# Layers 1 to 3 of a four-layer image network: one-level Strassen products on four PSUM pairs, attention in double steps, and reciprocals of gathered denominators

## The chip, the cores and the metric

The kernel runs on one core of a Trainium2 chip. A core has five engines that work side by side and wait for each other by semaphores: TensorE (PE) multiplies matrices out of SBUF into PSUM, VectorE (DVE) and ScalarE (ACT) work elementwise on SBUF and PSUM, GpSimd (POOL) works on SBUF, and SyncE (SP) issues transfers. PSUM has eight banks; a bank holds 512 float32 numbers in each of 128 partitions. The metric is the device time of one execution in microseconds, as the median of several runs. Everything is float32.

## The reference

The input x has 2 images of 512 channels and 32 x 32 pixels; each of four layers adds something to it. Layer 0 is attention with 64 sampled keys and a bias computed by a small network, followed by an MLP (512 to 2048 to 512); the change does not touch it. The three other layers, cut to what is computed:

```python
# layer 1: group norm, 8 heads of 64 channels, 1024 x 1024 scores per head
h = group_norm(x);  q, k, v = split(qkv_w @ h + qkv_b)
w = softmax(q.T @ k / 8);  x = x + proj_w @ (v @ w.T) + proj_b
# layer 2: group norm, one head of 512 channels
h = group_norm(x);  q, k, v = split(w_qkv @ h + b_qkv)
a = softmax(q.T @ k / sqrt(512));  x = x + w_proj @ (v @ a.T) + b_proj
# layer 3: no norm, queries and keys of 64 channels, values of 512
q, k, v = wq @ x + bq, wk @ x + bk, wv @ x + bv
x = x + gamma * (v @ softmax(q.T @ k, axis=1))
```

## The kernel before

The program is written out in full, without loops on the chip. The function `layers` runs after `layer0` and holds layer 0's MLP and then layers 1 to 3. A helper (`in_order`) makes each engine execute its instructions in the order in which they are written, so a wait at the head of an engine's queue holds everything behind it. Python generators (`advance`, `drain`) weave two pieces of work together in that order.

Channels lie on partitions, in four chunks of 128 (CC = 4), and the 1024 pixels of an image along the free dimension, in two halves of 512. `accumulate` (L135 in the profile) is a chain of matmuls into one PSUM region: each takes a 128 x 128 stationary block and a 128 x 512 moving block. The trace shows every matmul of the program as two records, because float32 goes through the array in two passes.

The order after the MLP is as follows.

- Layer 1: `project` (L1315, tile pm) makes queries and keys of two heads at a time with stationary blocks of 64 columns, in pairs on the two halves of the array; `values` (L135, pmv) makes the transposed values. The loop over 65 steps (image, pair of heads, block of 128 keys) writes the scores of one block for both heads (L1426, contraction over 64 rows, the two heads in pairs), takes exponentials on ACT (L1427), and multiplies the exponentials of the step before with the values (L1474, pv). DVE sums the exponentials (L1357). `divide` sums those over partitions with a matrix of ones (den, L1374), copies, inverts 128 x 1024 numbers (L1377) and multiplies. The next pair's projections and the output projection (`add_projection`, L1346) are woven into the steps.
- Layer 2 for each image: `project` with a folded weight g2 (t), `values` with a folded weight v2, eight score blocks (score2, L135) with exponentials (L1561), then `weigh` (pw2, L135): products of values and exponentials, each multiplied by the reciprocal of the denominators (L1532) and added to x (L1533).
- Layer 3 for each image: `project_both` (L1574), values, scores, `weigh`, and the store of the output.

PSUM is divided among three pools: two banks of `ps_m` for projections and the like, two pairs of banks for scores, one pair for pv. The MLP already uses one-level Strassen (Winograd's form with seven products and fifteen additions): `lefts`, `rights`, `products` and `combined`. There all seven products of a 128 x 128 output are written into two PSUM tiles before ACT and DVE read any of them. Before layer 3's end a `flag` is computed from the extreme reciprocals (`note`); if it is not zero, a slower general version of the three layers runs again.

Of the kernel before, what the change touches and what calls it, by code (L numbers as in the profile page):

```python
# [11 lines left out]
F32 = mybir.dt.float32  # L12
# [6 lines left out]
P = 128  # L19
B, C, H, W = 2, 512, 32, 32  # L20
HW = H * W
# [58 lines left out]
def kernel(ctx: ExitStack, tc: tile.TileContext, a: dict, out: bass.AP):  # L80
# [971 lines left out]
    def layers(f, fold_d, t2_b, o2_b):  # L1052
# [5 lines left out]
        chan = f.enter_context(tc.tile_pool(name="chan", bufs=4))  # L1058
        ps_m = f.enter_context(tc.tile_pool(name="ps_m", bufs=2, space=PSUM))
# [9 lines left out]
        NSUM = 12  # L1069
# [3 lines left out]
        def group_norm(x, gname, bname, out):  # L1073
# [9 lines left out]
            def over_group(v, name):  # L1083
                pg = ps_m.tile([P, CC], F32, name="pg", tag="mm")
                nc.tensor.matmul(pg, cs("gmean"), v, start=True, stop=True)
                g = small.tile([P, CC], F32, name=name)
                nc.vector.tensor_copy(g, pg)
                return g
# [25 lines left out]
            yield  # L1114
            for cc in range(CC):
                hc = chan.tile([P, HW], F32, name="hc", tag="chan")
                nc.gpsimd.tensor_scalar(  # L1117
                    hc, x[:, cc, :], sc[:, cc : cc + 1], sh[:, cc : cc + 1], ALU.mult, ALU.add
                )
                out.append(hc)  # L1120
            yield

        GN_STATS = CC + 3

        h1s, h2s = [[], []], [[], []]
        norm = group_norm(xs[0], "gn_w", "gn_b", h1s[0])
# [3 lines left out]
        with ExitStack() as mlp:  # L1130
# [124 lines left out]
            for blk in range(1, NBLK):  # L1255
# [21 lines left out]
                if blk + 1 < NBLK:  # L1277
                    right1 = normed_rights(blk + 1)
                else:
                    qkv1, proj1 = load_w(wa, "wa", [a["qkv1_w"], a["proj1_w"]])  # L1280
# [20 lines left out]
        drain(norm)  # L1301


        qkp = f.enter_context(tc.tile_pool(name="qkp", bufs=4))
        ps_s = f.enter_context(tc.tile_pool(name="ps_s", bufs=2, space=PSUM))
        ps_v = f.enter_context(tc.tile_pool(name="ps_v", bufs=1, space=PSUM))

        def project(w, lo, h, bias, r, wide):

            for half in range(2):  # L1310
                n = slice(half * HALF, (half + 1) * HALF)
                pm = ps_m.tile([P, HALF], F32, name="pm", tag="mm")
                for k in range(CC):
                    for at in range(0, P, wide):
                        nc.tensor.matmul(  # L1315
                            pm[at : at + wide],
                            w[:, k, lo + at : lo + at + wide],
                            h[k][:, n],
                            start=(k == 0),
                            stop=(k == CC - 1),  # L1320
                        )
                    if k == 1:
                        yield
                nc.scalar.activation(r[:, n], pm, AF.Identity, bias=bias)
                yield

        def values(w, h, vT, bias=None, scale=None):

            for s in range(8):
                pm = ps_m.tile([P, C], F32, name="pmv", tag="mm")  # L1330
                accumulate(pm, [(h[k][:, s * P : (s + 1) * P], w[:, k, :]) for k in range(CC)])
                if bias is not None:
                    nc.vector.tensor_add(vT[:, s, :], pm, bias)
                elif scale is not None:
                    nc.scalar.mul(vT[:, s, :], pm, scale)
                else:
                    nc.scalar.copy(vT[:, s, :], pm)
                yield

        def add_projection(x, w, bname, o):  # L1340
            for half in range(2):
                n = slice(half * HALF, (half + 1) * HALF)
                for m in range(CC):
                    pm = ps_m.tile([P, HALF], F32, name="ppr", tag="mm")
                    for k in range(CC):
                        nc.tensor.matmul(  # L1346
                            pm, w[:, k, m * P : (m + 1) * P], o[k][:, n], start=(k == 0), stop=(k == CC - 1)
                        )
                        if k == 1:
                            yield  # L1350
                    nc.vector.scalar_tensor_tensor(x[:, m, n], pm, col(bname, m), x[:, m, n], ALU.add, ALU.add)
                    yield

        def summed(acc, p, first):

            if first is None:
                nc.vector.tensor_add(acc, acc, p)  # L1357
            else:
                nc.vector.tensor_add(acc, first, p)  # L1359
# [6 lines left out]
        def divide(o, acc):  # L1366

            r = rp.tile([P, HW], F32, name="r")
            for half in range(2):
                n = slice(half * HALF, (half + 1) * HALF)  # L1370
                den = ps_m.tile([P, HALF], F32, name="den", tag="mm")
                for part in range(2):
                    q = slice(part * 64, part * 64 + 64)
                    nc.tensor.matmul(den[q], ones[:, :64], acc[:, part, n], start=True, stop=True)  # L1374
                nc.scalar.copy(r[:, n], den)
                yield
            nc.vector.reciprocal(r, r)  # L1377
            nc.vector.tensor_mul(o, o, r)
            note(r)
            yield  # L1380

        def reciprocals_of_both(acc):

            r = rp.tile([P, HW], F32, name="r")
            den = ps_v.tile([P, HW], F32, name="den2", tag="pv")
            for half in range(2):
                n = slice(half * HALF, (half + 1) * HALF)
                accumulate(den[:, n], [(ones, acc[:, part, n]) for part in range(2)])
                nc.scalar.copy(r[:, n], den[:, n])
                nc.vector.reciprocal(r[:, n], r[:, n])  # L1390
            return r

        wb_stack.close()
        fold2 = f.enter_context(tc.tile_pool(name="fold2", bufs=1))
        vbias = fold2.tile([P, C], F32, name="vbias")
        nc.sync.dma_start(out=vbias, in_=a["vb"][0].partition_broadcast(P))
        g2, v2 = [fold2.tile([P, CC, C], F32, name=name) for name in ("g2", "v2")]
        for w, j in ((g2, 0), (v2, 1)):
            nc.sync.dma_start(out=w, in_=fold_d[j])
        outs = f.enter_context(tc.tile_pool(name="outs", bufs=5))  # L1400

        vp = f.enter_context(tc.tile_pool(name="vp", bufs=1))
        pp_ = f.enter_context(tc.tile_pool(name="pp", bufs=4))
        accp = f.enter_context(tc.tile_pool(name="accp", bufs=1))
        rp = f.enter_context(tc.tile_pool(name="rp", bufs=1))

        def new_v():
            return vp.tile([P, 8, C], F32, name="vT")


        def qk1(h, m):
            q = qkp.tile([P, HW], F32, name="q", tag="qk")
            k = qkp.tile([P, HW], F32, name="k", tag="qk")
            yield (q, k)
            yield from project(qkv1, m * P, h, col("qkv_b", m), q, 64)
            yield from project(qkv1, C + m * P, h, col("qkv_b", CC + m), k, 64)

        def exponentials(qs, ks, left, scale):

            p = pp_.tile([P, 2, HW], F32, name="p")  # L1420
            for half in range(2):
                n = slice(half * HALF, (half + 1) * HALF)
                sc = ps_s.tile([P, 2, HALF], F32, name="score", tag="s")
                for part in range(2):
                    r = slice(part * 64, part * 64 + 64)
                    nc.tensor.matmul(sc[:, part, :], ks[part][r, left[part]], qs[part][r, n], start=True, stop=True)  # L1426
                nc.scalar.activation(p[:, :, n], sc, AF.Exp, scale=scale)  # L1427
            return p

        qk_steps = qk1(h1s[0], 0)  # L1430
        qk = next(qk_steps)
        drain(qk_steps)
        vT = new_v()
        drain(values(qkv1[:, :, 2 * C : 3 * C], h1s[0], vT, bias=vbias))
        norms = [
            group_norm(xs[1], "gn_w", "gn_b", h1s[1]),
            group_norm(xs[0], "gn2_w", "gn2_b", h2s[0]),
            group_norm(xs[1], "gn2_w", "gn2_b", h2s[1]),
        ]
        os_ = [[], []]  # L1440
        more = iter(())
        dividing = iter(())
        late = None
        for i in range(65):
            b, m, s = i // 32, i // 8 % 4, i % 8
            if i < 64:
                if s == 0:
                    if i:
                        drain(qk_steps)
                        qk = qk_next  # L1450
# [265 lines left out]
```

## Time and profile before

| | |
|---|---|
| median of 3 runs | 3491.22 us (3489.61 to 3491.63) |
| span of the profiled execution | 3487.9 us |
| layer 0 attention, up to 2160 us; MLP up to 2451.7 us | 2451.7 us |
| layers 1 to 3, 2451.7 us to the end | 1036.2 us |
| busy in the span: PE, DVE, ACT, POOL | 99%, 71%, 50%, 14% |

The profiled execution's span is 3.3 us under the median of the runs. A share of 99% for PE says that the array seldom waits, not that each of its instructions is needed; in layers 1 to 3 the waits of PE for other engines come to 7.4 us. The granted TensorE clock is 1.00 there (0.99 in the last stretch). All numbers of the prediction are made against the 3487.9 us span and carried over to the median by adding 3.3 us.

### The profile page before, as it was taken

How to read it: one execution, taken by the hardware profiler on the slowest of the kernel's cores; microseconds unless marked ns; L12 is line 12 of the kernel's file. 1: busy time of each engine (PE TensorE's matmuls, PEld its weight loads, DVE VectorE, ACT ScalarE, POOL GpSimd, SP SyncE). 2: the span in 40 equal slices, each digit the busy share in tenths (PEclk: the TensorE clock that was granted, in tenths of full speed). 3: DMA queues.
4: the chain of work that ended last, by engine and by line, in shares of the span. 5: the costliest groups of instructions: out<-in, count | busy, mean ns of one | idle time of the engine just before them, and what ended most of it. 6: DMA issues, size and time to landing. Idle time of an engine off the chain costs nothing.

```text
span 3487.9 us, 58691 instructions
## 1 busy us (share of the span) xinstructions
PE 3452.8 (99%) x24257; PEld 1446.9 (41%) x24257; DVE 2474.8 (71%) x2733; ACT 1754.7 (50%) x2479; POOL 491.4 (14%) x579
## 2 busy tenths in 40 slices
PE   9999999999999999999999999999999999999999
PEld 4333333333333233333333369999433333444443
DVE  6999999999997999999999845455264374130223
ACT  4767867867765867768676612112243242011111
POOL 0222222222221222222222200000001000000000
PEclk9999999999999999999999999999999999999999
DMA  5776676666774666766676620001000000000000
GB/s 167 151 148 143 135 154 140 148 146 139 150 149 91 145 147 131 151 141 143 151 149 141 135 95 10 13 13 56 34 1 0 1 0 0 15 0 0 6 30 25
DMA packets 134068, 313.65 MB, mean 90 GB/s; under 512 B 21152, under 2 KB 66592, under 8 KB 133024
## 3 DMA queue, kind: packets, MB, share of 16 engines
q0 software_dynamic: 56880, 199.79, 30.1%
q1 hardware_dynamic: 75616, 105.31, 9.5%
q8 instruction: 193, 3.16, 0.4%
q10 hardware_dynamic: 1296, 4.72, 0.3%
q14 instruction: 83, 0.68, 0.1%
HBM read 65.17 MB, written 10.75 MB: 22 GB/s over the span
## 4 chain that ended last, share of the span: by engine, by line
PE 78%; DVE 16%; issue 4%; ACT 2%; DMA 0%; POOL 0%; DVEq 0%; SPq 0%; ACTq 0%; POOLq 0%
PE z L542 33%; PE pw L135 6%; DVE wa L525 6%; PE pm L1315 5%; PE pma L135 5%; PE pmv L135 5%; DVE h L556 5%; PE pmb L135 4%; PE score L1426 4%; PE score L135 3%; PE pv L1474 3%; DVE h L525 2%; PE ppr L1346 2%; PE pmp L135 2%; PE pp L628 1%
## 5 line engine op out<-in xcount | busy, mean ns | idle before, releaser
L542 PE MATMUL z<-wa,cpb_w 128*32 128x512 f32 x11904 | 1779.1, 593 | 6.6 <-DVE simbias L489 3.4
L551 ACT ACTIVATE h<-z,b2h 128x1024 f32<-128x1024 f32 x1024 | 1134.4, 1114 | 529.7 <-PE z L542 506.2
L542 PE MATMUL z<-h,cpb_w 128*32 128x512 f32 x4480 | 986.3, 593 | 3.3 <-ACT h L551 2.2
L525 DVE CUSTOM_DVE_ANT_1 wa<-tab,tab 128x1024 f32<-128x1024 f32 x744 | 878.4, 1216 | 34.0 <-PE z L542 33.9
L542 PEld LDWEIGHTS z<-wa,cpb_w 128*32 128x32 f32 x11904 | 492.9, 110 | 883.7 <-issue 805.5
L556 DVE SCALAR_TENSOR_TENSOR h<-h,turn,h 128x1024 f32<-128x1024 f32 x512 | 653.5, 1276 | 8.8 <-ACT h L551 8.6
L542 PEld LDWEIGHTS z<-h,cpb_w 128*32 128x32 f32 x4480 | 256.3, 110 | 335.0 <-issue 291.8
L831 POOL DMA_DIRECT2D h<-h x255 | 226.5, 888 | 1071.0 <-DVE h L556 697.4
L525 DVE CUSTOM_DVE_ANT_1 h<-tab,tab 128x1024 f32<-128x1024 f32 x280 | 333.0, 1216 | 10.5 <-PE z L542 10.4
L1427 ACT ACTIVATE p<-score 128x1024 f32<-128x1024 f32 x144 | 139.5, 1021 | 184.8 <-PE score L1426 184.8
L135 PE MATMUL pw<-p,vT 128*128 128x512 f32 x512 | 221.8, 593 | 1.3 <-DVE y L1532 1.3
L1357 DVE TENSOR_TENSOR acc<-acc,p 128x2048 f32<-128x2048 f32 x56 | 128.8, 2300 | 105.1 <-ACT p L1427 57.8
L1210 ACT COPY p<-pma 128x128 f32<-128x128 f32 x70 | 18.5, 265 | 304.2 <-PE pma L135 304.2
L824 POOL DMA_DIRECT2D h<-h x126 | 108.7, 863 | 343.5 <-DMA h<-h 339.8
L1359 DVE TENSOR_TENSOR acc<-p 128x2048 f32<-128x2048 f32 x12 | 27.5, 2291 | 182.4 <-ACT p L1561 108.8
L135 PEld LDWEIGHTS pw<-p,vT 128*128 128x128 f32 x512 | 97.0, 190 | 122.6 <-issue 121.0
L1202 DVE TENSOR_TENSOR upper<-pma,p 128x256 f32<-128x256 f32 x70 | 29.5, 422 | 163.3 <-ACT p L1210 163.3
L828 POOL DMA_DIRECT2D h<-h x126 | 121.9, 968 | 117.9 <-DMA h<-h 111.4
L1426 PE MATMUL score<-q,k 64*128 64x512 f32 x512 | 127.2, 615 | 0.0
L1117 POOL TENSOR_SCALAR hc<-x,sc,sh 128x1024 f32<-128x1024 f32 x16 | 27.5, 1728 | 704.4 <-DVE sh L1113 507.8
L1315 PE MATMUL pm<-hc,wa 128*64 128x512 f32 x512 | 122.4, 603 | 0.0
L1474 PE MATMUL pv<-p,vT 128*64 128x512 f32 x512 | 121.4, 595 | 0.0
(320 smaller groups left out, 3239.7 us busy)
## 6 DMA issues: line engine op xcount, KB each, us to landing
h<-h POOLq DMA_DIRECT2D x255, 512.0 KB, 4.8
h<-h POOLq DMA_DIRECT2D x252, 256.0 KB, 4.9
tab<-slog_d SPq DMA_DIRECT2D x128, 256.0 KB, 4.5
h<-h SPq DMA_DIRECT2D x126, 256.0 KB, 2.3
xt<-in_xt SPq DMA_DIRECT2D x8, 512.0 KB, 7.6
wa<-in_mlp_w SPq DMA_DIRECT2D x4, 1024.0 KB, 7.9
wb<-in_mlp_w SPq DMA_DIRECT2D x16, 256.0 KB, 5.6
x_d<-x SPq DMA_DIRECT2D x32, 128.0 KB, 1.8
```

Of the source, the lines that this page charges most:

```text
L135: nc.tensor.matmul(pm, w, m, start=(k == 0), stop=(k == len(pairs) - 1))
L525: nc.vector._custom_dve(TENSOR_ADD_SAT, out=h1.rearrange("p (y x) -> p y x", x=W), in0=tx[:, quad, point, :].unsqueeze(1).to_broadcast([P, ...
L542: nc.tensor.matmul(z[point * 32 : point * 32 + 32, n], cpb_w2[:, lo : lo + 32], h1s[point][:, n], start=True, stop=True,)
L551: nc.scalar.activation(h2, z, AF.Relu, bias=b2h[:, part : part + 1])
L556: nc.vector.scalar_tensor_tensor(h2, h2, turn[:, part // 2 : part // 2 + 1], parts.pop(part + 1), ALU.mult, ALU.add)
L828: nc.gpsimd.dma_start(out=joins[i - 3][1:P:2], in_=joins.pop(i - 2)[1:P:2], accum_op=ALU.add)
L831: nc.gpsimd.dma_start(out=joins[i - 1], in_=other, accum_op=ALU.add)
L1315: nc.tensor.matmul(pm[at : at + wide], w[:, k, lo + at : lo + at + wide], h[k][:, n], start=(k == 0), stop=(k == CC - 1),)
L1357: nc.vector.tensor_add(acc, acc, p)
L1426: nc.tensor.matmul(sc[:, part, :], ks[part][r, left[part]], qs[part][r, n], start=True, stop=True)
L1427: nc.scalar.activation(p[:, :, n], sc, AF.Exp, scale=scale)
L1474: nc.tensor.matmul(pv[part * 64 : part * 64 + 64, n], vT[:, ls, lo : lo + 64], lp[:, part, n], start=(ls == 0), stop=(ls == 7),)
```

## The change

Layer 0 and the MLP keep their instructions, but for the way in which layer 1's weights are loaded. Layers 1 to 3 are rewritten:

- Every large product except the per-head attention is split one level by Strassen: the two operands are cut into 2 x 2 blocks, sums of blocks are formed (`left_sums`, `right_sums`, eight additions), and seven block products replace eight. `group` does one such unit. It takes two PSUM tiles of two banks each, xy and vz (regions x, y, v, z of one bank each), out of a pool of four such pairs, which now serves everything. In `group`, ACT copies x (p1) after the first product and v (p5) after the third, DVE adds u2 and u3, and further products accumulate onto what lies in x, y and v. The moving block is 512 wide (n = HALF) in q/k, t and output projections, and 256 wide (n = QUARTER) in values, score2, pw2 and pw3. The first unit of layer 1 is done without Strassen (`plain`).
- The projections of all heads come before the attention of an image, with 128-column stationary blocks. `attend` has 17 steps of two key blocks; its scores use the four pairs too.
- `divide` copies the sums, moves one row per head into a compact 128 x 16 tile by DMA, inverts that, writes it to DRAM and reads it back spread over 64 partitions.
- In layers 2 and 3 the sums of exponentials are added on GpSimd (`grow`). In layer 3 the exponentials are divided before the sums of blocks are formed (`shared`): GpSimd multiplies four 128 x 1024 tiles, and DVE forms four additions for each.
- The work is staggered by hand: for instance `shared` stands between the two units of a weighed product.

```diff
-        ps_s = f.enter_context(tc.tile_pool(name="ps_s", bufs=2, space=PSUM))
-        ps_v = f.enter_context(tc.tile_pool(name="ps_v", bufs=1, space=PSUM))
...
+        banks = f.enter_context(tc.tile_pool(name="banks", bufs=4, space=PSUM))
...
+        def pair(name):
+            return banks.tile([P, 2, HALF], F32, name=name, tag="pair")
...
+        def right_sums(b11, b12, b21, b22, t1, t2, t4, t3=None):
+
+            nc.vector.tensor_tensor(t1, b12, b11, ALU.subtract)
+            nc.vector.tensor_tensor(t2, b22, t1, ALU.subtract)
+            nc.vector.tensor_tensor(t4, b21, t2, ALU.subtract)
+            nc.vector.tensor_tensor(b12 if t3 is None else t3, b22, b12, ALU.subtract)
...
+        def group(name, nk, n, stationary, moving, evict, plain=False):
+
+            xy, vz = pair(name), pair(name)
+            x, y, v, z = xy[:, 0, :n], xy[:, 1, :n], vz[:, 0, :n], vz[:, 1, :n]
...
+            add(x, 0, 0)
+            p1 = temp("p1", n)
+            nc.scalar.copy(p1, x)
+            add(y, 5, 5)
+            u2 = temp("u2", n)
+            nc.vector.tensor_tensor(u2, y, p1, ALU.add)
+            add(v, 4, 4)
+            p5 = temp("p5", n)
+            nc.scalar.copy(p5, v)
+            add(z, 3, 3)
+            add(x, 1, 1, False)
+            add(y, 6, 6, False)
+            u3 = temp("u3", n)
+            nc.vector.tensor_tensor(u3, y, p1, ALU.add)
+            add(v, 2, 2, False)
+            evict((x, None), (v, u2), (z, u3), (p5, u3))
...
+            for i in range(17):
+                m, sp = divmod(i, 4)
...
+                    for s in (2 * sp, 2 * sp + 1):
+                        for half in range(2):
+                            n = slice(half * HALF, (half + 1) * HALF)
+                            sc = pair("score")
...
+                            nc.scalar.activation(p, sc, AF.Exp, scale=64 ** -0.5)
...
+            nc.vector.reciprocal(few, few)
+            note(few)
+            d = sums_d.tile([P, HW // 64], F32, name="d")
+            nc.sync.dma_start(out=d, in_=few)
...
+            def grow(self, c):
+                p = self.score(c)
+                self.p.append(p)
...
+                    nc.gpsimd.tensor_tensor(self.acc, self.p[0] if c == 1 else self.acc, p, ALU.add)
+
+            def divisor(self):
...
+                accumulate(den, [(ones, acc[:, k]) for k in range(2)])
+                self.r = temp("r", HALF)
+                nc.vector.reciprocal(self.r, den)
+                note(self.r)
+
+            def normalize(self, c):
+                y = self.p[c].rearrange("p (k n) -> p k n", k=2)
+                nc.gpsimd.tensor_tensor(y, y, self.r.unsqueeze(1).to_broadcast([P, 2, HALF]), ALU.mult)
...
+            def form(self, c):
...
+                right_sums(*self.parts(c))
...
+            def shared(self):
+                self.divisor()
+                for c in range(4):
+                    self.normalize(c)
+                for c in range(4):
+                    self.form(c)
...
+                def evict(c11, c12, c21, c22):
+                    q = [p[:, i * QUARTER : (i + 1) * QUARTER] for i in range(4)]
+                    nc.scalar.activation(q[0], c11[0], AF.Exp, scale=C ** -0.5)
+                    put(q[2], c21)
+                    put(q[3], c22)
+                    put(q[1], c12)
+                    nc.scalar.activation(p[:, QUARTER:], p[:, QUARTER:], AF.Exp, scale=C ** -0.5)
...
+        steps = weighed("pw3", xs[0], 0, seven_v, a0, gb3, store(0))
+        advance(steps)
+        a1.shared()
+        seven_x = pixels3(xs[1])
+        both = project_both(xs[1])
+        drain(steps)
...
+        steps = weighed("pw3", xs[0], 1, seven_v0, a1, gb3, store(0))
+        advance(steps)
+        b0.shared()
+        drain(steps)
+        for c in range(4):
+            b1.grow(c)
+        steps = weighed("pw3", xs[1], 0, seven_v, b0, gb3, store(1))
+        advance(steps)
+        b1.shared()
+        checks = guard()
+        advance(checks)
+        drain(steps)
+        steps = weighed("pw3", xs[1], 1, seven_v, b1, gb3, store(1))
```

## The prediction

> **What bounds the kernel now.** I read first the busy time by stage (columns: stretch in us, its length, then busy us of PE, PEld, DVE, ACT, POOL, granted clock, DMA share, GB/s), with stages cut where the chain of waits changes its lines.
>
> ```profile
> 2451.70:2493.30 41.60, 41.60 (x131) 16.64 (x130) 7.10 (x13) 4.30 (x6) 0.00 (x0) 1.00 0.17 64
> 2493.30:2908.50 415.20, 411.85 (x1673) 135.57 (x1673) 234.09 (x161) 157.62 (x179) 17.64 (x8) 1.00 0.00 1
> 2908.50:2991.10 82.60, 82.60 (x194) 36.68 (x194) 15.29 (x11) 10.76 (x17) 0.00 (x0) 1.00 0.00 0
> 2991.10:3276.70 285.60, 282.87 (x663) 124.83 (x663) 61.95 (x71) 31.86 (x40) 4.72 (x4) 1.00 0.02 5
> 3276.70:3487.90 211.20, 203.83 (x530) 84.83 (x530) 56.17 (x54) 34.30 (x44) 0.00 (x0) 0.99 0.08 26
> ```
>
> Layers 1 to 3 take 1036.2 us and PE is busy in 1022.8 of them: PE's own instructions bound the stage, and DVE and ACT have much room. The chain in order of time gives their rates, free of overlap (start, us, line, records):
>
> ```profile
> 2433.86 5.36 PE pmb L135 x48
> ...
> 2493.28 1.92 PE score L1426 x8
> 2495.19 1.87 PE pm L1315 x8
> ...
> 2506.35 1.72 PE pv L1474 x8
> ...
> 3057.32 34.35 PE pw L135 x80
> ```
>
> Two records are one matmul: 0.859 us for a moving block of 512 (34.35/40), 0.223 for 128 (5.36/24), so 0.43 for 256 by the line between them. A score matmul costs 0.48, a pv one 0.43, a 64-column projection 0.467.
>
> Last, the order of time around the one place where PE writes the second bank of a two-bank tile after ACT has read the first:
>
> ```profile
> 3326.51 1.88 PE L135 MATMUL den<-acc,ones 128*128 128x512 f32 x4
> ...
> 3328.43 0.58 ACT L1389 COPY r<-den 128x512 f32<-128x512 f32 x1 [7.89 <-PE den L135]
> ...
> 3329.07 1.98 PE L135 MATMUL den<-acc,ones 128*128 128x512 f32 x4 [0.68 <-ACT r L1389]
> ...
> 3330.89 3.17 PE L135 MATMUL pw<-p,vT 128*128 128x512 f32 x7
> ```
>
> PE waits although the banks differ. Eight records took 4.38 us (3326.51 to 3330.89) where 8 x 0.429 = 3.43 are needed: **one such round trip costs 0.95 us**, 0.585 of it the copy.
>
> **The change part by part.**
>
> *1. Fewer products.* Before, the PE rows of layers 1 to 3 add up to 1019: q/k 256 x 0.467 = 119.7; values 165; t and output projections 110; score2 110; pw 220; attention scores, pv and den 248; layer 3's scores and projections 29; den of layers 2 and 3 17.5. After, I count in the built order 226 matmuls of 512 (193.9), 1008 of 256 (432.4), 288 scores (138.2), 256 pv (110), 32 den (15.4), 16 wide den (13.7) and 32 projections of layer 3 (14): 917.6. Saved: 102 us. A 256-wide matmul costs at least 0.429 (half of 512) and, held up by its weights, at most 2 x 0.223 = 0.446: up to 17 us for the range.
>
> *2. New round trips.* In the built order the first matmul of y waits for the copy p1 that reads x, and the first of z for p5 that reads v: these are the two banks of one tile, as in den above. PE stands still twice in each of 71 units. Fifteen units have n = 512: 30 x 0.95 = 28.5. Fifty-six have n = 256; ACT's PSUM copy takes 0.265 at 128 and 0.585 at 512, so 0.37 at 256, and a trip 0.95 - 0.21 = 0.74: 112 x 0.74 = 82.9. Sum: **111.4 us**. A unit of n = 256 and two blocks then takes 6.02 + 1.48 = 7.5 against 6.87 for the eight products that it replaces. The ends are 73 (the idle time alone, 0.68 at 512 and so 0.47 at 256) and 135 (0.95 for each of the 142).
>
> *3. Exponentials in front of p1.* In score2 ACT's queue holds the exponential of 768 elements (0.85, between 0.50 for 256 and 1.02 for 1024) before the next unit's p1, and it waits for three DVE additions (3 x 0.42) after the unit's last matmul. It ends 2.35 after that matmul; p1 could have started at 1.0. So +1.4 for each of 16 units: 22 us (13 to 30).
>
> *4. `shared`, four times.* DVE's queue: eviction of the unit before (3 x 0.42 and 2 x 0.75, so 3), reciprocal of 512 (3.32), two reductions (0.7 each), then 16 additions of 256 (0.42) that wait for four GpSimd products, and only then u2 of the second unit, for which PE's x waits. A GpSimd tensor-by-tensor operation has no row. The nearest is a one-input pass over 128 x 1024, from the POOL's order of time:
>
> ```profile
> 2418.99 5.10 POOL L1117 TENSOR_SCALAR hc<-x,sc,sh 128x1024 f32<-128x1024 f32 x4 [41.46 <-DVE sh L1113]
> ...
> 2868.91 8.63 POOL L1117 TENSOR_SCALAR hc<-x,sc,sh 128x1024 f32<-128x1024 f32 x4 [239.14 <-DVE sh L1113]
> ```
>
> That is 1.28 alone and 2.16 beside DVE's two-input sums. Lower bound 1.28 (same speed), upper 4.3 (both inputs at the contended rate); I take two uncontended passes, 2.55. Then u2 is ready 3 + 3.3 + 4 x 2.55 + 1.7 + 0.4 = 18.6 after the first unit's end; PE could use it at 1.7 (den) + 4 x 1.72 + 2 x 0.74 = 10.1. It waits 8.5, and about 10 with additions and products in each other's way; the a1 call has 7 us of other PE work ahead but 5 of pixel sums on DVE. In all 38 us (17 to 72).
>
> The Trainium skill, GPSIMD Engine Reference, "Performance versus the Vector engine", gives 4497 ns for a two-input addition of 2048 float32 elements, so an estimate of 2.25 us for 1024, which would make part 4 about 5 us smaller; it advises VectorE for such work, which speaks against this part of the change. Its page SBUF — State Buffer, "Who interferes with whom", says that a GpSimd instruction reading SBUF and a VectorE one with two SBUF inputs exclude each other; the 2.16 beside 1.28 agrees, and full exclusion would add some 5 us per call.
>
> *5. Attention in double steps.* Scores, pv and den cost PE the same. A double step is 3.84 + 3.44 = 7.3 us of PE; in it ACT has four exponentials (4.1), DVE four additions (4 x 1.19 = 4.8), so both stay covered, and three score pairs beside pv suffice: the fourth score starts at 2.9, the first exponential ends at 2.2. Start and end: 2.5 for each image. The value bias moves from DVE (16 x 0.69) to GpSimd behind the division: nothing, since the next unit waits for it only in part 7.
>
> *6. Compact inversion.* Removes 8 x 6.55 of reciprocals and 8 x 2.4 of reductions from DVE, nearly all beside PE; before, it showed as 2.2 us of waiting at 2906. It adds five DMAs per pair on SP's queue, which has nothing else there, but DVE's product now waits at the head of its queue for two trips (landing 2 to 4.5 us each by the page's rows). In `attend` one double step lies between: zero. After the last pair in the second image only one value unit does: 4 us.
>
> *7. Seams.* Beginning with the MLP's last tiles 1; sums of value blocks before each of four weighed products 1.7 each; den between score units, with its reciprocal on DVE, 4.5 per image; pixel sums and group norm 2.2; loading of layer 3's weights behind the release of layer 2's is covered by a 13.5 us unit. With parts 5 and 6: 28 us (10 to 60). The tail after the last product, 6.2 before, stays.
>
> *Sum:* 917.6 + 111.4 + 22 + 38 + 28 + 6 = 1123, against 1036.2: +87. Span 2451.7 + 1123 = 3574.7; plus 3.3 for the median: **3578 us**.
>
> Part 4's waits are the longest; before, the longest wait of PE here is 2.2 us, and the granted clock stays at 1.00 or 0.99. The Trainium skill, TensorE: Matmul & The Clock Gate, "The HAM clock gate", says that the clock halves after an idle window of some 3.4 us; no run here shows it, and by it an estimated 2 us per call would come on top, 3586.
>
> **Rivals.** A, my forecast: the round trips eat the saving (102 against 111) and the rest is loss. B, faster: the copies hide, because a wait on the other bank is not paid as in den. Then 917.6 + 22 + 38 + 28 + 6 = 1012, 24 us less, 3467. For it speaks that ACT is idle most of the stage; against it den's row, and that the copy alone lasts 0.37. It decides where a trip costs under 0.17 us: (111.4 - 87)/142. C, much slower: GpSimd products at 4.3 and in DVE's way, so that `shared` costs 18 each and score units stretch by 2: 1123 + 34 + 32 = 1189, 3644. D, the flag fires and the general layers run too: thousands of us; the data give no reason. E, the split saves less than it says (256-wide products held up by weight loads): 17 us more, 3595, inside the range.
>
> **How the numbers follow.** A with E 0.75, C 0.15, B 0.09, D 0.01. A and E alone: part 1 up to 17, part 2 from 73 to 135, part 3 from 13 to 30, part 4 from 17 to 72, part 7 from 10 to 60. All low give 1037 and all high 1238, 3492 and 3693; they are independent, so half of each distance, 3535 to 3635. Taking in half of C makes 3525 to 3640; below it lies B, above it the worst of C and D. A kernel like this is told from no change beyond about 0.2% (7 us): faster 0.08, same 0.03, slower 0.89.
>
> **What would show it.** Right: PE idle in layers 1 to 3 rises from 13 us to over 150; PE waits for p1 and p5 head the list of waits, 71 each, 0.5 to 0.7 us idle; score2 units start 8.9 us apart, value units 7.5; DVE works through `shared` while PE waits for u2 four times. Wrong: y starting right after x; GpSimd products near 1.3; PE busy well above 930.

## The result and the profile after

The changed kernel takes 3609.03 us (median of 4 runs, 3607.79 to 3612.62), the kernel before 3490.57 (3489.61 to 3491.63): a ratio of 1.0341, 95% interval 1.0326 to 1.0356. It is slower by 118 us; the forecast was 3578, 87 slower. The profiled execution has a span of 3606.0 us, of which layers 1 to 3 take 1154.7 instead of 1036.2.

Busy time by stage of the changed kernel (columns as in the prediction; rows 1 and 2: projections and attention of the first image; 3 and 4: the first output projection, then the same of the second image; 5 and 6: the second output projection and layer 2; 7: the end of layer 2 and layer 3):

```profile
2451.30:2539.60 88.30, 77.92 (x231) 42.12 (x230) 31.41 (x50) 12.80 (x26) 0.00 (x0) 1.00 0.01 3
2539.60:2661.10 121.50, 121.15 (x541) 42.70 (x540) 84.77 (x101) 70.51 (x76) 20.28 (x7) 1.00 0.08 23
2661.10:2782.40 121.30, 105.87 (x292) 52.96 (x290) 37.58 (x65) 16.26 (x30) 7.31 (x4) 0.99 0.03 7
2782.40:2903.90 121.50, 121.15 (x541) 42.72 (x540) 91.53 (x109) 69.30 (x74) 24.56 (x10) 1.00 0.10 31
2903.90:2980.60 76.70, 66.25 (x178) 31.18 (x177) 31.87 (x53) 10.31 (x18) 7.28 (x4) 1.00 0.03 7
2980.60:3290.00 309.40, 248.44 (x975) 181.02 (x975) 161.97 (x304) 48.94 (x107) 43.85 (x20) 0.98 0.02 5
3290.00:3606.00 316.00, 242.22 (x986) 174.76 (x986) 162.82 (x256) 41.37 (x77) 67.39 (x29) 0.92 0.05 17
```

Before, PE was busy in 99% of layers 1 to 3; now it stands still in every stage except attention, for 171.7 us in all (1154.7 less 983.0), and in the last stage it also runs at a lower clock. The waits of PE there (total us, times, longest):

```profile
PE pw L1356 <- DVE u L1376: 45.5, 5, 12.5
PE score L1356 <- ACT p L1373: 23.8, 16, 6.1
PE pmv L1356 <- ACT p L1373: 14.1, 24, 1.5
PE pmv L1356 <- ACT p L1379: 11.9, 24, 0.5
...
PE score L1356 <- ACT p L1379: 7.8, 16, 0.5
PE pw L1356 <- DVE vs L1332: 7.0, 7, 1.8
```

All lines with p together (L1373 is p1, L1379 is p5) make 95.5 us in 142 waits; u makes 59.0, of which `shared` has 44.8 in four waits of 12.5, 8.6, 11.3 and 12.5 us. One unit of values in order of time shows both round trips; 12 of the last row's 16 records are its own, so the next unit starts at 2516.7 and this one takes 7.56 us (forecast 7.5):

```profile
2509.13 1.03 PE L1356 MATMUL pmv<-wa,hc 128*128 128x256 f32 x4
2510.67 1.99 PE L1356 MATMUL pmv<-wa,h1t 128*128 128x256 f32 x8 [0.52 <-ACT p L1373]
2513.13 1.13 PE L1356 MATMUL pmv<-wa,h1t 128*128 128x256 f32 x4 [0.46 <-ACT p L1379]
2514.10 3.62 PE L1356 MATMUL pmv<-wa,hc 128*128 128x256 f32 x16
```

And one call of `shared`, first POOL's line, then DVE's, then PE's:

```profile
3335.85 9.61 POOL L1767 TENSOR_TENSOR p<-p,r 128x1024 f32<-128x1024 f32 x4 [14.06 <-DVE r L1762]
```
```profile
3332.42 3.35 DVE L1762 RECIPROCAL r<-den 128x512 f32<-128x512 f32 x1
...
3338.24 2.55 DVE L1338 TENSOR_TENSOR pt<-p 128x256 f32<-128x256 f32 x1 [1.16 <-POOL p L1767]
3340.82 2.44 DVE L1339 TENSOR_TENSOR pt<-p,pt 128x256 f32<-128x256 f32 x1
3343.30 2.45 DVE L1340 TENSOR_TENSOR pt<-p,pt 128x256 f32<-128x256 f32 x1
3345.67 0.41 DVE L1341 TENSOR_TENSOR p<-p 128x256 f32<-128x256 f32 x1
...
3350.76 0.42 DVE L1376 TENSOR_TENSOR u<-pw,p 128x256 f32<-128x256 f32 x1
```
```profile
3336.74 1.99 PE L1356 MATMUL pw<-pt,vT 128*128 128x256 f32 x8 [0.52 <-ACT p L1379]
3351.24 6.19 PE L1356 MATMUL pw<-p,vT 128*128 128x256 f32 x16 [12.51 <-DVE u L1376]
```

PE waits 12.5 us for one addition of 0.42 us that stands behind everything else in DVE's queue. While GpSimd multiplies (9.61/4 = 2.4 us each), DVE's additions last 2.44 to 2.55 us instead of 0.42. After the wait the 16 records of PE take 6.19 us; in the value unit above, 16 took 3.62.

### The profile page after: what moved, and what is told of

Read it like the earlier page. It is cut to its first block, busy times and chain, and to the rows that moved or that the text cites. A ratio compares the mean times of both kernels' runs of the same rounds, so it can differ in the third digit from the quotient of the medians.

```text
span 3606.0 us, 61030 instructions
## 1 busy us (share of the span) xinstructions
PE 3413.1 (95%) x24805; PEld 1615.9 (45%) x24805; DVE 2701.4 (75%) x3360; ACT 1785.3 (50%) x2600; POOL 639.6 (18%) x640
## 4 chain that ended last, share of the span: by engine, by line
PE 70%; DVE 19%; issue 6%; ACT 4%; POOL 1%; DMA 0%; DVEq 0%; SPq 0%; ACTq 0%; POOLq 0%
PE z L542 32%; DVE wa L525 6%; PE pma L135 5%; DVE h L556 4%; PE pmb L135 4%; PE pmv L1356 4%; PE pw L1356 4%; PE pv L1514 3%; PE score L1500 3%; PE pm L1356 3%; DVE h L525 2%; PE score L1356 2%; PE pmp L135 2%; PE pp L628 1%; PE pmt L1356 1%
## 5 line engine op out<-in xcount | busy, mean ns | idle before, releaser
L1504 ACT ACTIVATE p<-score 128x1024 f32<-128x1024 f32 x128 | 120.6, 1033 | 76.8 <-PE score L1500 76.4
L1356 PE MATMUL pw<-p,vT 128*128 128x256 f32 x384 | 97.5, 408 | 45.5 <-DVE u L1376 45.5
L1535 DVE TENSOR_TENSOR acc<-acc,p 128x1024 f32<-128x1024 f32 x96 | 114.2, 1251 | 27.8 <-ACT p L1504 27.8
L1500 PE MATMUL score<-q,k 64*128 64x512 f32 x512 | 118.5, 602 | 0.7 <-ACT p L1504 0.7
L1356 PE MATMUL pmv<-wa,hc 128*128 128x256 f32 x384 | 94.4, 390 | 16.1 <-DVE u L1376 8.1
L1356 PEld LDWEIGHTS pw<-p,vT 128*128 128x128 f32 x384 | 77.9, 206 | 65.5 <-DVE u L1376 47.5
L1567 POOL TENSOR_SCALAR o<-o,vb 128x1024 f32<-128x1024 f32 x8 | 30.7, 3832 | 401.9 <-DVE o L1566 231.8
L512 ACT ACTIVATE tab<-tab,pc 128x512 f32<-128x512 f32 x126 | 96.2, 763 | 0.0
```

The source lines that it names most:

```text
L1356: nc.tensor.matmul(out, stationary(l, k), moving(r, k), start=start and k == 0, stop=k == nk - 1, skip_group_check=not start,)
L1500: nc.tensor.matmul(sc[:, part, :], ks[m][r, s * P : (s + 1) * P], qs[m][r, n], start=True, stop=True)
L1504: nc.scalar.activation(p, sc, AF.Exp, scale=64 ** -0.5)
L1535: nc.vector.tensor_add(acc[half], acc[half], ps[s, half])
```

## The experiments

The kernel before had medians of 3490.1 to 3491.6 us beside these runs, so its time moved by 0.04%. "Slow clock" in the table counts the groups of 256-wide records in layers 1 to 3 that ran over by more than 0.3 us: what they took beyond 0.216 us for each record and 0.17 at the group's end. Waits are PE's, from the profiled execution of each.

| run | median us | waits for p | waits for u | slow clock |
|---|---|---|---|---|
| the change | 3609.0 | 95.5 | 59.0 | 16.6 |
| e1 other pairing | 3587.2 | 9.3 | 123.6 | 49.1 |
| e2 `shared` spread | 3579.1 | 95.8 | 28.2 | 14.3 |
| e3 exponential behind p1 | 3600.8 | 81.3 | 62.1 | 21.2 |
| e9 product on DVE | 3599.0 | 95.4 | 47.5 | 18.1 |
| e5 = e1 + e2 + e3 | 3533.0 | 2.9 | 84.0 | 34.0 |
| e6 = e5, forms two late | 3528.8 | 2.9 | 78.3 | 30.7 |
| e4 eight products | 3474.1 | 0 | 0 | 0 |
| e7 eight, no sums | 3477.5 | 0 | 0 | 0 |
| e8 seven where DVE is free | 3456.9 | 0.8 | 18.7 | 5.1 |
| e10 = e8, sums behind u2 | 3444.1 | 0.8 | 7.5 | 0 |

**1. The other pairing of the banks.**

```diff
-            xy, vz = pair(name), pair(name)
-            x, y, v, z = xy[:, 0, :n], xy[:, 1, :n], vz[:, 0, :n], vz[:, 1, :n]
+            xv, yz = pair(name), pair(name)
+            x, v, y, z = xv[:, 0, :n], xv[:, 1, :n], yz[:, 0, :n], yz[:, 1, :n]
```

> One line of `group` is changed: x and v share a two-bank tile, and y and z the other; every instruction stays and keeps its place. Theory (round trips): y then need not wait for p1, nor z for p5; the copies run beside the product on the other tile. The 142 waits of 0.46 to 0.73 us for p1 and p5 go, with 111.4 us by the forecast's prices; up to 0.1 us each may come back where v waits for p1 or z for u2 (14 us), and the score units lose a part of what the late p1 costs (10 of 22). 95 to 125 us faster than the changed kernel, 3484 to 3514. Rival 1 (the stops belong to the array's change of bank or of operands, and the trace only puts the copy's name on them): less than 20 us faster, above 3589. Rival 2 (the gaps only move, to u2 and u3): 20 to 60 us faster, with as many waits for u as there were for p.

Measured: 3587.2 us (3582.0 to 3588.5), 22 us faster than the change, where the theory asked for 95 or more. The mechanism was right, though: without any change of order the waits for p fell from 95.5 to 9.3 us, and a value unit runs through in 6.05 us instead of 7.56:

```profile
2506.97 3.62 PE L1356 MATMUL pmv<-wa,hc 128*128 128x256 f32 x16
2510.43 2.75 PE L1356 MATMUL pmv<-wa,h1t 128*128 128x256 f32 x12
2513.02 3.62 PE L1356 MATMUL pmv<-wa,hc 128*128 128x256 f32 x16
2516.47 2.75 PE L1356 MATMUL pmv<-wa,h1t 128*128 128x256 f32 x12
```

So a trip costs (7.56 - 6.05)/2 = 0.755 us (forecast 0.74), and it belongs to the tile, not to the bank or to the array. PE's idle time is 0.49 of it. The other 0.27 is 0.17 at the end of the group before the wait and 0.10 because the records after it start slower (8 of them take 1.99 us instead of 1.89). PE's stops for u and vs in the change pay the same 0.27. The Trainium skill, PSUM — Partial Sum Buffer, "PSUM bank collisions raise a hardware error", says that accesses of two engines to different banks run clean; this run agrees, since ACT now copies out of one bank beside PE's product in another: the wait came from the program, which orders accesses by tile.

What the theory missed is rival 2, though not in its form: there are 31 waits for u, up to 15.4 us long, not as many as there were for p. In layers 2 and 3 PE now comes earlier to a DVE that is no earlier: the waits for u rise by 64.6 us. And the clock falls more often: in this kernel's score units of layer 2, 12 records behind waits of 0.40 and 1.98 us take 4.6 us, and the granted clock (the column before the last two) is 0.50 for 3.4 us there,

```profile
3171.56 1.13 PE L1356 MATMUL score<-ts,h2t 128*128 128x256 f32 x4 [0.40 <-ACT p L1373]
3174.67 1.53 PE L1356 MATMUL score<-t,h2t 128*128 128x256 f32 x4 [1.98 <-DVE u L1376]
3176.00 3.22 PE L1356 MATMUL score<-t,hc 128*128 128x256 f32 x8
```
```profile
3175.30:3178.70 3.40, 3.40 (x10) 2.69 (x9) 0.00 (x0) 0.00 (x0) 0.00 (x0) 0.50 0.00 0
```

where 8 such records take 1.89 at full clock. The account closes to 2 us: 86.2 less of waits for p, 30 less at 114 fewer stops (0.27 each), 64.6 more for u, 32.5 more of slow clock, 1.2 more of others: 18 us less, against 19.3 between the two profiled spans.

**2. `shared` spread over later units.** DVE's additions (`form`) leave `shared`; a0's and a1's go behind the value units that follow, b0's and b1's behind the units of the product before, whose calls start one unit earlier.

```diff
             def shared(self):
                 self.divisor()
                 for c in range(4):
                     self.normalize(c)
-                for c in range(4):
-                    self.form(c)
...
         for c in range(4):
             advance(value_steps)
+            a0.form(c)
             a1.grow(c)
```

> `shared` now holds only the denominators and the four GpSimd products; DVE's sixteen additions stand behind later units, by ones or twos, and the last two calls begin one unit earlier. Theory (DVE's queue holds u2 behind additions that wait for GpSimd): the four waits of 8.6 to 12.5 us for u2 (44.8 us) and the slow clock after each (16 records in 5.2 to 6.2 us instead of 3.6, so 8.6 us) go; up to 3 us each may come back where a product starts before the last sums are there: 40 to 53 us faster than the changed kernel, 3556 to 3569. Rival (the work of GpSimd and DVE itself is the limit, since the two exclude each other, and the wait moves to the next product): 0 to 15 us faster, above 3594, with waits of 8 us or more elsewhere.

Measured: 3579.1 us (3576.2 to 3581.0), 30 us faster; neither theory nor rival. Three of the four long waits went, and waits of 0.4 to 2.1 us stand in their place. One of 9.6 us stayed, in the product with a1, whose u2 stands behind sums of value blocks and b0's denominators, and its cause is what the rival said. DVE's order of time in this kernel, while GpSimd multiplies (3474.13 to 3483.9):

```profile
3475.28 1.48 DVE L1331 TENSOR_TENSOR wa<-vT 128x256 f32<-128x256 f32 x1
3476.80 2.44 DVE L1332 TENSOR_TENSOR wa<-wa,vT 128x256 f32<-128x256 f32 x1
3479.28 2.44 DVE L1333 TENSOR_TENSOR wa<-vT,wa 128x256 f32<-128x256 f32 x1
3481.65 2.56 DVE L1334 TENSOR_TENSOR vT<-vT 128x256 f32<-128x256 f32 x1
3484.13 0.41 DVE L1331 TENSOR_TENSOR wa<-vT 128x256 f32<-128x256 f32 x1
```

These are sums of value blocks that wait for nothing of GpSimd's, and each still takes as long as one GpSimd product. So two causes add up in `shared`: the place in DVE's queue, and that DVE's additions of two SBUF operands get through only between GpSimd's instructions.

**3. The exponential behind p1.**

```diff
-                    nc.scalar.activation(p[:, QUARTER:], p[:, QUARTER:], AF.Exp, scale=C ** -0.5)
+                    pending.append(
+                        lambda: nc.scalar.activation(p[:, QUARTER:], p[:, QUARTER:], AF.Exp, scale=C ** -0.5)
+                    )
...
             nc.scalar.copy(p1, x)
+            while pending:
+                pending.pop(0)()
```

> In layer 2's score units the exponential of 768 elements, and the addition of the tile on GpSimd, are written behind the copy p1 of the next unit. Theory (ACT's queue holds p1 behind an exponential that waits for DVE): score units fall from 8.5 us to about 7.3; 16 times 1.4 is 22 us, 16 to 26 us faster than the changed kernel, 3583 to 3593. Rival (p1 waits for something else, as the release of PSUM or of temporary tiles): 0 to 6 us faster, above 3603.

Measured: 3600.8 us (3600.5 to 3604.6), 8 us faster: between the theory's 16 to 26 and the rival's 0 to 6. The theory's cause holds and its size does not. Undisturbed score units fall from 8.5 to 7.55 us, because PE's wait for p1 falls from 1.46 to 0.52 us: p1 was late by 0.94 us, not by 1.4, and in 11 score units, not in all 16. In all, 14 us of waits for p went, and 3 us of waits for u and 5 us of slow clock came. One wait for p1 of 6.1 us, which was a single event beside the group norm of the second image, fell to 4.0. ACT's order of time in the changed kernel says why:

```profile
3046.41 0.84 ACT L1824 ACTIVATE p<-p 128x768 f32<-128x768 f32 x1 [1.15 <-DVE p L1397]
3047.28 1.28 ACT L1102 ACT_TABLE_LOAD   x1
3050.42 0.21 ACT L1102 ACTIVATE rs<-var 128x4 f32<-128x4 f32 x1 [1.86 <-DVE var L1099]
3050.64 1.28 ACT L1103 ACT_TABLE_LOAD   x1
3051.94 0.21 ACT L1103 ACTIVATE rs<-rs 128x4 f32<-128x4 f32 x1
3052.05 0.35 ACT L1373 COPY p<-score 128x256 f32<-128x256 f32 x1
```

The copy p1 stands behind two functions of the norm with a table load of 1.28 us each, and the first of them waits for DVE, whose addition was just held up for 2.56 us beside GpSimd's sum of exponentials.

**4. Eight products.** `group` always takes its branch without p1, p5, u2 and u3; the fourth sum of each set, which overwrites an operand, is not formed. In this kernel the two off-diagonal blocks of the value units and of layer 2's score units stand in each other's place; the amount of work is the same.

```diff
-            if plain:
+            if True:
```

> All units use the branch `plain`: eight block products instead of seven, no p1, p5, u2 and u3, and of each four sums of blocks the three that overwrite nothing are still formed, though not read. Theory: PE gets 27 us more of 512-wide and 62 us more of 256-wide matmuls, and loses 111 us of round trips, 22 us of late p1 and 54 us of `shared` (nothing of the next unit waits on DVE): 90 to 125 us faster than the changed kernel, 3484 to 3519, so that Strassen's form costs here more than the eighth product that it saves. Rival (the loss lies in the restaging, the sums and the seams, not in the form of the unit): about 89 us slower, 3680 to 3700, or between the two.

Measured: 3474.1 us (3472.8 to 3475.7): 135 us faster than the change, 10 more than the theory's upper end, and faster than the kernel before (ratio 0.9953, 0.9936 to 0.9970). PE waits 2.9 us in all of layers 1 to 3:

```profile
PE pm L1354 <- DVE upper L1207: 2.2, 1, 2.2
PE score L1499 <- ACT p L1503: 0.7, 2, 0.3
```

So Strassen's form as written costs here 135 us more than it saves, and the restaging (the new order of projections, attention and divisions) is no loss. The table accounts for it: waits for p 95.5, waits for u 59.0, 7 of other waits, 44 at 166 fewer stops (0.27 each) and slow clock 16.6, less 89 for the eighth products, make 133 of the 133.6 us between the two profiled spans.

**5 and 6. The three edits together, and the forms later still.** The sixth run also moves, in `score_blocks`, each `form` one score unit further back.

> The edits of the first three experiments together. Alone they took 22, 30 and 8 us off the changed kernel (3609), so by addition 3549. Theory (with the other pairing PE no longer waits for ACT's copies but for DVE, whose queue holds u2; in that run the waits for u rose from 59 to 122 us, 64 of them in pw): the spread sums of `shared` then free more than alone, because PE comes to them earlier: pw's waits fall from 64 to some 20 us, and the slow clock after the waits goes with them: 3515 to 3535. Rival (the pairing only exposes DVE's total work, which stays): 3545 or more.

> As the run before (three together), and in layer 2 the four additions on a tile of exponentials stand two score units behind it instead of one. Theory: the fourth addition overwrites a block that GpSimd's sum of exponentials still reads, so it waits for GpSimd (2.2 to 2.6 us in the trace) with u2 of the unit behind it on DVE; two units later the sum has been made: the waits of score and pmv for u (53 us in the run with the other pairing alone) fall by 25 to 40 us with the clock that they cost, so 25 to 40 us faster than the run before. Rival (DVE is stopped whenever GpSimd works, wherever the additions stand): 0 to 8 us faster.

Measured: 3533.0 us (3528.4 to 3533.9) and 3528.8 (3528.1 to 3530.2). Together the edits give 76 us, where their single gains add up to 60: the theory's range held. But 84 us of waits for u stayed, and those of pw fell to 34 us, not to 20. The sixth run was to free the addition that overwrites what GpSimd still reads; it gave 4 us, within its rival's range: the waits for u fell by 5.7 us, and those for sums of value blocks rose by 4.8 (one is 8.2 us long). In DVE's order of time of that run a plain pair of score units reads

```profile
2993.97 0.42 DVE L1388 TENSOR_TENSOR u<-score,p 128x256 f32<-128x256 f32 x1 [2.95 <-PE score L1358]
...
2996.84 0.42 DVE L1341 TENSOR_TENSOR p<-p 128x256 f32<-128x256 f32 x1
2997.18 0.16 DVE L1091 COPY mean<-mv 128x4 f32<-128x4 f32 x1
2997.25 0.42 DVE L1380 TENSOR_TENSOR u<-score,p 128x256 f32<-128x256 f32 x1
```

From the start of one unit's u3 to the end of the next one's u2 are 3.70 us, with three evictions and four additions between and no wait; PE comes for u2 after 3.4 (it waited 0.33). There is no room left, so each reciprocal with its reductions (4.7 us) and each piece of the group norm (1.5) shows as a wait. What bounds the score units without round trips is the work on DVE between u3 and u2, not the one wait for GpSimd.

**7. Eight products and no sums.**

> Eight products in all units, with the blocks of the transposed units in their right places, and no sums of blocks at all. Theory: PE alone bounds such a kernel, DVE's sums were hidden already: 3474 as with the unused sums, within 4 us, and 0.3 to 0.6% faster than the kernel before: that is what the restaging is worth without Strassen's form. Rival (the sums cost PE something by sharing SBUF): 3455 to 3468.

Measured: 3477.5 us (3475.0 to 3478.1), ratio to the kernel before 0.9960 (0.9946 to 0.9974). DVE has 258 us of work instead of 422 in run 4, and the time is the same to 3 us: what DVE does costs nothing where no product waits for it. PE's rows alone make this kernel: 1006.6 by the prediction's prices (917.6, and an eighth product for 15 units of 512 and 56 of 256, 89), measured 1021.9 with 2.9 of waits and 7.5 of tail, so the products take 0.5% more than priced.

**8. Seven products only where DVE has room.** Units for queries, keys, t, output projections and values keep seven products, with the pairing of run 1; scores of layer 2 and the weighed products take eight.

```diff
-            if plain:
+            if plain or name in ("score2", "pw2", "pw3"):
```

> Strassen's form, with x and v in one pair of banks, only in the units for queries, keys, t, output projections and values; eight products and no sums in layer 2's scores and in the weighed products, where DVE's queue is full. Theory: against eight products everywhere (3474), 15 units save 2 x 0.859 and 24 units 2 x 0.43, in all 46 us, and give back some 10 in waits for u: 3428 to 3445, and so 1.3 to 1.8% faster than the kernel before. Rival (a unit of seven has a loss of its own beyond the trips): 3460 to 3480.

Measured: 3456.9 us (3454.3 to 3458.9), ratio 0.9899 (0.9883 to 0.9916). That is 20 us faster than run 7, where the theory's 3428 to 3445 would be 32 to 49, and it lies between the theory and the rival: 18.7 us of waits for u and 5.1 of slow clock came back, twice what was allowed for. The longest, 4.7 us, is again a u2 behind sums of blocks (four for the attention outputs and four for the projection's weights).

**9. The product of `shared` on DVE.** One word: `nc.gpsimd` becomes `nc.vector` in `normalize`.

> The changed kernel, with the four products of `shared` on DVE instead of GpSimd. In the trace of the changed kernel, from the reciprocal's end to u2 takes 15.4 us: 9.6 for GpSimd's four products, in which DVE gets only three of its additions done (2.5 us each instead of 0.42), then the rest. Theory (GpSimd's own time, and DVE shut out beside it): on DVE it is 2 x 0.7 of reductions, 4 x 1.23, 16 additions in some 5.9 and 0.4, so 12.6: 2.8 us less for each of four calls, and a little of the slow clock: 10 to 16 us faster than the changed kernel, 3593 to 3599. Rival (the product reads its second operand by a broadcast and is slow on DVE too, or GpSimd's time was hidden): within 4 us of it, 3605 to 3613, or slower.

Measured: 3599.0 us (3598.1 to 3602.3), 10 us faster, at the theory's lower end. DVE's order of time in this kernel:

```profile
3338.52 4.62 DVE L1767 TENSOR_TENSOR p<-p,r 128x1024 f32<-128x1024 f32 x4
3343.06 0.42 DVE L1338 TENSOR_TENSOR pt<-p 128x256 f32<-128x256 f32 x1
```

Four products take 4.62 us there and 9.61 on GpSimd, and no addition is held up. The four waits of `shared` are still 5.7 to 9.6 us, 33 of 44.8 in all, so the place in the queue is the larger part.

**10. Sums behind u2.** As run 8; the steps that were woven in behind a unit are written behind the next unit's u2.

```diff
             nc.vector.tensor_tensor(u2, y, p1, ALU.add)
+            behind_u2()
...
-                for steps in between:
-                    advance(steps)
+                behind.extend(lambda steps=steps: advance(steps) for steps in between)
```

> As the run with seven products where DVE is free, but the sums of blocks and the divisions that are woven between the units of projections and values are written behind u2 of the next unit, instead of ahead of it. Theory (u2 is late because sums stand ahead of it in DVE's queue, as in `shared`): the waits of pmv and pm for u, 18.7 us with 4.7 the longest, go to under 5, and the slow clock behind them too: 12 to 22 us faster than that run (3457), 3435 to 3445. Rival (the sums are late for the product after, and the waits move there): within 5 us of it.

Measured: 3444.1 us (3443.6 to 3449.7), 13 us faster than run 8 and the best of all: ratio to the kernel before 0.9874, interval 0.9857 to 0.9890. What is left of the waits for u is 7.5 us (the theory said under 5), and one wait of 1.9 us is new, for sums that now come late for their own product:

```profile
PE pmv L1370 <- DVE u L1393: 7.5, 5, 2.5
PE ppr L1370 <- DVE ot L1347: 1.9, 1, 1.9
```

The two longest, 2.5 us each, are a u2 behind the reciprocal of den and its two reductions (4.7 us on DVE), which stay ahead of it here.

## Why the prediction was right, and where its sum was short

The direction, the main mechanism and the range held. The sum for layers 1 to 3 was 1123 and the profile has 1154.7; term by term, in us (parts 3 and 6 were too dear by some 4 us each, which hid as much of what part 4, the seams and the clock cost beyond the sum):

| part | forecast | measured |
|---|---|---|
| 1 products | 917.6 | 921, by difference |
| 2 round trips | 111.4 | 116: 78 idle and 142 x 0.27 |
| 3 late p1 | 22 | 12, and 5.6 at the group norm |
| 4 `shared` | 38 | 53.4: 44.8 idle and 8.6 slow clock |
| 5 to 7 attention, inversion, seams | 28 | 39: 24 of waits, 8 slow clock, 7 at the 27 other stops |
| tail | 6 | 7.5 |

- *Part 1* held within 0.4%, and so did its count: the trace has 2016 records of 256-wide products, two for each of the 1008 matmuls. Run 7 shows the prices almost without waits.
- *Part 2*, the step that carries the forecast, was right in count (142 waits), in price (0.755 against 0.74) and in cause: the row of den, where PE waited for the other bank of the same tile, was the same thing in the kernel before. Rival B asked that copies hide; run 1 shows that they do so once the tiles are paired otherwise, so B failed for the reason that the den row gave.
- *Part 3* was mis-sized: p1 was late by 0.94 us, not 1.4, and in 11 score units and two value units behind them instead of 16. The 5.6 us at the group norm are more than the 2.2 that part 7 has for pixel sums and norm together; the prediction had not looked at what stands in ACT's queue between the score units, or it would have found the two table loads.
- *Part 4* was right in mechanism, and its price for a GpSimd product (2.55) near the measured 2.44; the estimate of 2.25 that the prediction made from the Trainium skill, GPSIMD Engine Reference, "Performance versus the Vector engine", was a little further off, from below. The term that was too small is "about 10": the waits were 8.6 to 12.5. The prediction let the four additions of each tile overlap GpSimd's next product, and in the trace they hardly do. It had named that exclusion and priced it at some 5 us per call in a sentence on the Trainium skill's page SBUF — State Buffer, "Who interferes with whom", without taking it into the sum. By the rows shown, from the reciprocal's end to that of u2 the prediction has 12.3 us and the trace 15.4, so it cost 3.1 us in the call shown.
- *The slow clock*, likewise named from the Trainium skill, TensorE: Matmul & The Clock Gate, "The HAM clock gate", and left out of the sum, cost 1.6 to 2.6 us after each call (the estimate was 2), and 8 us elsewhere, which no term had.
- *Parts 5 to 7*: attention ran at 7.22 us a double step (forecast 7.3), 121.5 us an image with GpSimd and ACT covered, and the inversion cost PE nothing (forecast 4): DVE's product waited for its transfers once, 1.3 us, beside PE's work. The longest wait among the value units, 2.85 us, is a u2 behind eight sums of blocks, the same cause as in run 8. What is left of parts 5 to 7 was 15 us dearer than forecast, 8 of them slow clock behind waits of 1 to 6.1 us.

Of the signs that the prediction named, value units came 7.56 us apart (7.5) and score units 8.5 (8.9). "PE busy well above 930" came true although the forecast did: 983, since PE's busy time in the profile contains the slow clock (16.6) and 0.27 us at each of 169 stops (45), part of which the prediction had counted in the trips.

## What to carry to other kernels

A saved product is worth its own time only if everything that the next product waits for comes from an engine with a short queue: before forming sums for a Strassen step, add up what stands on DVE and ACT between a product's end and the next one's need, and write the short operation that PE waits for ahead of the bulk. When a consumer reads one PSUM region while PE writes the next, put the two regions in different tiles, if the waits are set by tile as here; two changed lines removed 86 us of waits for p. And taking one wait away is measured only with the next one: run 1 alone gave 22 us, with the other two edits the three gave 76, and Strassen's form kept only where DVE has room, with u2 ahead of the sums, gave 165.

## What the runs showed of the hardware

- Short waits can slow PE, not only long ones. In run 1 six waits of 1.8 to 2.0 us, one per score unit of the second image or right behind them, were each followed by 12 records that took up to twice their time: 1.8 us lost each (of 49.1 in that run), and the granted clock is 0.50 for 3.4 us behind the one shown. Waits of 0.5 us twice in 7.5 us left the clock alone in the change. In run 6 two waits of 1.7 us and in run 10 two of 2.5 us had no such effect, so the length of the wait does not settle it; what does stays open. The Trainium skill, TensorE: Matmul & The Clock Gate, "The HAM clock gate", names an idle window of some 3.4 us; the waits here that were followed by slow records are shorter, and the measurement decides.
- GpSimd and DVE get in each other's way, and either can lose: DVE's additions took 2.4 to 2.6 us beside GpSimd's products (0.42 alone), and GpSimd's one-input pass over 128 x 1024 beside DVE's sums in attention took 3.83 us on average, where the same size took 1.28 alone in the trace of before:

```profile
L1567 POOL TENSOR_SCALAR o<-o,vb 128x1024 f32<-128x1024 f32 x8 | 30.7, 3832 | 401.9 <-DVE o L1566 231.8 <-ACT p L1504 170.1
```

- A product of a 128 x 1024 tile with the 128 x 512 reciprocals, read twice, takes 2.4 us on GpSimd and 1.16 on DVE (4.62/4).
